# One more key and value group made early, the last block of one thread split by batch, and a new written-out order

## The chip, the cores and the metric

The kernel runs on one core of one Trainium2 chip. The time is device microseconds of one execution. The engines are PE (matmul), DVE (vector), ACT (activation functions), POOL (GpSimd) and SP, which here only issues transfers. Each engine works through its own instructions strictly in the order in which the program holds them, and waits on semaphores for the others. All data are float32; the profile records two PE passes for each float32 matmul.

## The reference

Eight batches of 128 tokens with 256 features pass four transformer blocks, one after the other; a context of the same shape is read by the cross-attentions.

```python
# L0: cross-attention to ctx (16 heads of 16), MLP with tanh gelu
x = x + attn(ln(x), ctx) ; x = x + gelu_tanh(ln(x) @ fc) @ proj
# L1: the context is the "x" of a perceiver block, the stream its latents:
#     keys and values from ctx and the stream together, masked; rms norm, MLP
# L2: twice, i = 1, 2: cross-attention with 16 heads of 128 each
h  = ln_i(x)
q, k, v = h @ wq_i + bq_i, ctx @ wk_i + bk_i, ctx @ wv_i + bv_i     # 256 -> 2048
k, v = concat(k, bias_k_i), concat(v, bias_v_i)                     # one learned key
x  = x + softmax(q k / sqrt(128)) v @ wo_i + bo_i
x  = x + gelu_erf(ln(x) @ w_fc1) @ w_fc2                            # MLP m2
# L3: causal self-attention (a4), cross-attention (a5), MLP with tanh gelu (m3)
x  = x + attn(ln1(x), ln1(x), mask) ; x = x + attn(ln2(x), ctx) ; x = x + mlp(ln3(x))
```

## The kernel before, in words

**Threads.** The batches are dealt to four threads of two batches each, T0 to T3. `blocks(T)` (L1362) is the whole life of a thread: attention a0 and MLP m0 (L0), a1 and m1 (L1), the wide attention twice (L2, `wide_attention`, L1163), m2, then a4, a5 and m3 (L3), and the store of its rows. T2 starts when T0 has left L1, T3 when T1 has left L1 and T0 has left its wide attentions. So the narrow blocks of one thread, which need much of DVE and ACT, stand beside the wide attention of another, which needs mostly PE.

**The wide attention.** `group(T, i, hg)` (L1232) makes four of the 16 heads: `queries` and `keys_values` (L1172) project, two heads to a product of 256 columns; values are one 128x512 product for a batch. Keys go to "kb" buffers (20), values to "vw" (4). `after_scores` (L1302) is the softmax of one batch's four heads in a "t" buffer (7 of them, 128x516, shared with the narrow attentions), the transposes, the weighted values and the output product. Keys and values need only the context. `AHEAD` (L63) names the groups whose keys and values a thread makes at its very start, beside a0 and m0; the `loader` (L510) fetches their weights right after those of a0. A thread may hold four weight buffers of 512 KB (`NW`), all threads eleven.

**Norms.** `normed` and `norm` (L569, L585) make the statistics, and `root` (L608): ten tiny DVE operations that compute the reciprocal square root; then the scaling (either ACT or DVE), transposes on PE through a "tl" bank, and the copy out. POOL adds the bias row to x.

**Products.** `proj`, `product` and `taken` (L541 to L712): a product takes one of two "mm" PSUM banks, PE fills it, then ACT or DVE empty it and the bank is free. `mlp` (L717) does this with gelu on ACT. Scores of the narrow attentions take the four "sc" banks; small transposes and softmax products the two "tl" banks. In L3, `by_pairs` (L1041) makes the softmax with rows of four exponentials on ACT, each with an accumulated sum; in L0 and L1, `by_keys` (L916) uses maxima per key (the tiles "mp") instead. At most two narrow attentions are under way at a time (`attn_lock`).

**What sets the order.** Nothing is ordered at run time. While the program is built, class `Plan` (L83) plays the threads as coroutines: each operation asks for an engine with an urgency (the table `U`, plus the thread's lateness for the stage from `LATE`, smaller is sooner); when the planned engine is free, the most urgent operation gets it and is written to that engine's instruction list. `_weight` (L263) holds the planned duration of each kind of operation, `dma` (L412) that of a transfer. So costs, urgencies and latenesses alter the order of the instructions and nothing else. When PE has nothing to do in the plan and its planned clock is about to fall, `idle_work` (L397) puts in a matmul of the identity with itself, "idle-filling matmul" below, whose result nobody reads.

Every engine call goes through one wrapper, so all of them carry line L333 in the profile; tiles tell the operations apart. Names: "w" weights, "hT" normalised and transposed rows, "ctxT" the transposed context, "kb" keys, queries and hidden rows, "at" and "attnT" attention outputs, "xn" normalised rows, "st", "mv", "rv", "ry", "rz" the parts of the norm, "sm" and "mn" softmax sums and maxima.

Of the kernel before, what the change touches and what calls it, by code (L numbers as in the profile page):

```python
# [18 lines left out]
P = 128  # L19
# [43 lines left out]
AHEAD = [[(1, 0), (1, 1)], [], [], []]  # L63
U = {'take': -0.44, 'taken': -1, 'norm': -0.47, 'mask': 0.26, 'k': 2.41, 'q': 1.79, 'v': 2.5, 'by key': 0.5, 'softmax': 2.46, 'weights': 1.63, 'pairs': 0.75, 'out': 1.79, 'mlp norm': 0.75, 'mlp 1': 4.29, 'mlp 2': 1.92, 'wide norm': -1, 'wide k': 3.49, 'wide q': 4.0, 'wide v': 4.43, 'wide s': 1.19, 'wide': -0.3, 'ahead': 4.34, 'load': -0.39}
LATE = [(1.69, 2.1, 2.22, -0.57, 1.75, 0.04, 2.53, 1.2, 4.53, 1.81), (12.77, 7.95, 10.47, 7.4, 1.7, -1, 8.48, 3.14, 7.46, 6.32), (3.27, 2.62, 3.89, 0.6, 2.14, -1, 4.58, 4.56, 5.62, 0.26), (0.03, 1.69, 0.31, 1.11, 0.24, 3.18, -0.81, -0.64, -0.7, 1.05)]
# [17 lines left out]
class Plan:  # L83
# [12 lines left out]
    def __init__(self):  # L96
        self.now = 0
        self.seq = 0
        self.events = []
        self.asked = []  # L100
        self.until = {e: 0 for e in self.SEEN}
        self.weight, self.shared, self.wrote = 0, False, []
        self.idle_work = None
        self.both_until = {"DVE": 0, "POOL": 0}
        self.clock = Clock()
        self.count = 0
        self.log = []
        self.table = None
        self.dma_until = 0
        self.live = {}  # L110
# [152 lines left out]
def _weight(eng, name, args, kw):  # L263
# [3 lines left out]
    n = max(sizes)  # L267
# [21 lines left out]
    if eng == "DVE":  # L289
        if name == "tensor_scalar" and n == 4 and len(aps) == 2 and len(args) > 5:  # L290
            return 145, False
        if name == "reciprocal":
            return 65 + 6.25 * n, False
        if name in ("bn_stats", "bn_aggr"):
            return (330 if name == "bn_stats" else 150), False
        if n <= 8:
            return 68, False
        if name in ("tensor_scalar", "tensor_copy") and on_sbuf:
            return 75 + 0.8 * n + 55 * by_part, True
        two = name in ("tensor_tensor", "scalar_tensor_tensor") and sum(  # L300
            x.space == bass.MemoryType.SB and x.free_size() > 1 for x in aps[1:]) == 2
        return 72 + 1.03 * n + 55 * by_part, two
# [35 lines left out]
class Engines:  # L338
    def __init__(self, nc, plan):
        self.tensor, self.vector = Engine(nc.tensor, plan, "PE"), Engine(nc.vector, plan, "DVE")  # L340
        self.scalar, self.gpsimd = Engine(nc.scalar, plan, "ACT"), Engine(nc.gpsimd, plan, "POOL")
        self.sync = nc.sync


def op(eng, f, lat=None, table=None):
    return ((eng, 480 if eng == "SP" else 0, f, lat, table),)
# [8 lines left out]
def four_blocks(ctx: ExitStack, tc: tile.TileContext, a: dict, out: bass.AP):  # L355
# [56 lines left out]
    def dma(f, kb_, early):  # L412

        yield op("SP", lambda: f(nc.sync)) + (op("ACT", lambda: f(nc.scalar)) if early else ())
        plan.dma_until = max(plan.dma_until, plan.now) + kb_ * 2.8
        yield plan.dma_until - plan.now + 2300
# [36 lines left out]
    class Thread:  # L453
        def __init__(self, h, b0, nb):
            self.h = h
            self.nb, self.nt = nb, nb * P
            self.batches, self.tokens = slice(b0, b0 + nb), slice(b0 * P, (b0 + nb) * P)
            self.x = new(const, [P, nb, D], f"x{h}")
            self.ctx = ctxT[:, :, self.tokens]
            self.ready = Event()  # L460
            self.row_in = Event()
            self.w_slots = Slots(NW)
            self.w = {}
            self.w_in = {}
            self.late = 0.0
            self.ahead = {}

# [42 lines left out]
    def loader(T):  # L510
        names = list(weight_list())
        first = {f"l{i}{hg}{x}" for i, hg in AHEAD[T.h] for x in "kv"}
# [23 lines left out]
    def drop(T, n=1):  # L536
        plan.put(T.w_slots, n)
        plan.put(w_slots, n)
# [46 lines left out]
    def norm(T, src, e, w, b, adds, rows, hT, ready, row_done, urgency):  # L585
# [4 lines left out]
        else:  # L590
# [17 lines left out]
            def root():  # L608
# [11 lines left out]
                if b is not None:  # L620
                    nc.vector.tensor_tensor(z, mean, v, ALU.mult)

# [540 lines left out]
    def wide_attention(T, i):  # L1163
        hT, hT_in = yield from normed(
            T, T.x, 1e-5, f"L2_ln{i}_scale", f"L2_ln{i}_offset", [(T.x, T.x, f"L2_bo{i}")], U["wide norm"] + T.late)
        for hg in range(4):
            ends = yield from group(T, i, hg, hT, hT_in)
# [4 lines left out]
    def keys_values(T, i, hg, step_back):  # L1172

        n = f"l{i}{hg}"
        ks, vs = [], []
        bv = []
# [4 lines left out]
        def keys():  # L1181
# [3 lines left out]
            for m in range(0, 4, 2):  # L1185
                yield (kb_slots, 2)
                two = [kb(), kb()]
# [15 lines left out]
        def values():  # L1203
# [3 lines left out]
            for b in range(nb):  # L1207
                yield (v_slots, 1)
                t = new(act, [P, 512], "vw", bufs=4)
# [20 lines left out]
        return ks, vs, k_in, v_in  # L1230

    def group(T, i, hg, hT, hT_in):  # L1232
# [32 lines left out]
        ks, vs, k_in, v_in = T.ahead.pop((i, hg), None) or keys_values(T, i, hg, late)  # L1265
# [3 lines left out]
        for b in range(nb):  # L1269
# [9 lines left out]
            ends.append(spawn(after_scores(T, i, hg, b, s, vs, v_in[b], n), U["wide"] + late, Plan.SEEN["PE"]))  # L1279
        plan.put(kb_slots, 8)  # L1280
# [21 lines left out]
    def after_scores(T, i, hg, b, s, vs, v_in, n):  # L1302
# [59 lines left out]
    def blocks(T):  # L1362
# [6 lines left out]
        for i, hg in AHEAD[h]:  # L1369
            T.ahead[i, hg] = keys_values(T, i, hg, LATE[h][0] + U["ahead"])  # L1370
# [27 lines left out]
        T.late = LATE[h][7]  # L1398
# [4 lines left out]
        T.late = LATE[h][8]  # L1403
# [4 lines left out]
        T.late = LATE[h][9]  # L1408
# [66 lines left out]
```

## Time and profile before

| | us |
|---|---|
| median of 3 runs | 1197.38 (1197.1 to 1198.49) |
| the profiled execution | 1198.46 |
| its span | 1196.7, so 1.76 lie outside |
| PE, DVE, ACT, POOL busy | 1145.7, 751.2, 574.1, 339.1 |
| granted PE clock, mean | 0.996 |
| first wide query product of T0 | 177.3 |
| end of T3's wide attention, end of its m2 | 1028.4, 1069.4 |
| one table load on ACT, count | 1.283, 50 |
| 512 KB of weights, issue to landing | 3.9 |

A matmul's length in the profile is its way through the array; the next one starts sooner, so for PE the distance from start to start tells the cost. A line of the view by stretch has the time from and to, its length, then busy time and instructions of PE, weight loads, DVE, ACT and POOL, the granted clock, the share of time that the DMA engines were busy, and GB/s. Times count from the start of the span.

### The profile page before, as it was taken

What the parts mean: (1) busy time and instruction counts of PE and PEld (TensorE: products, weight loads), DVE (VectorE), ACT (ScalarE), POOL (GpSimd) and SP (SyncE); (2) the same over time, 40 slices, a digit from 0 to 9 for tenths busy, and PEclk for the clock granted to TensorE, in tenths of its full rate; (3) what the DMA queues carried; (4) which work ended last, traced back from release to release, by engine and by line L of the source; (5) the groups of instructions that cost most, each with busy time, mean ns of one, the idle gap of its engine ahead of it and who ended that gap; (6) DMA issues with size and microseconds to landing.
All of it is one profiled execution on the core that took longest, in us unless ns stands there. A gap on an engine that the chain in (4) does not pass through costs nothing.

```text
span 1196.7 us, 21922 instructions
## 1 busy us (share of the span) xinstructions
PE 1145.7 (96%) x8318; PEld 937.0 (78%) x8318; DVE 751.2 (63%) x1943; ACT 574.1 (48%) x1448; POOL 339.1 (28%) x392
## 2 busy tenths in 40 slices
PE   8899889999999999999999999999999999999888
PEld 7577668788887777787888897787887887877767
DVE  7755668744554867977872365626568456778872
ACT  4344544452433345675653243434436334686972
POOL 4021111112221210360611022211217212475870
PEclk9899999999999999999999999999999999999999
DMA  9423131336444324343324644543544543432120
GB/s 319 131 84 116 54 98 58 125 117 191 131 147 132 107 90 130 103 133 97 118 85 130 190 145 121 161 157 125 145 130 141 159 133 111 134 100 67 51 80 18
DMA packets 107321, 145.59 MB, mean 122 GB/s; under 512 B 6736, under 2 KB 66256, under 8 KB 107216
## 3 DMA queue, kind: packets, MB, share of 16 engines
q1 hardware_dynamic: 105984, 143.02, 38.3%
q8 instruction: 66, 1.08, 0.4%
q10 hardware_dynamic: 1232, 1.16, 0.3%
q14 instruction: 39, 0.32, 0.1%
HBM read 143.11 MB, written 1.05 MB: 120 GB/s over the span
## 4 chain that ended last, share of the span: by engine, by line
PE 78%; DVE 13%; ACT 5%; issue 1%; POOL 1%; DMA 0%; ACTq 0%; POOLq 0%; DVEq 0%
PE mm L333 57%; PE tl L333 17%; PE sc L333 5%; DVE t L333 2%; DVE mp L333 1%; DVE rz L333 1%; ACT t L333 1%; ACT pt L333 1%; DVE mn L333 1%; ACT q L333 1%; POOL t L333 1%; DVE ry L333 1%; DVE q L333 1%; ACT L333 1%; DVE rv L333 1%
## 5 line engine op out<-in xcount | busy, mean ns | idle before, releaser
L333 PE MATMUL mm<-hT,w 128*128 128x256 f32 x1216 | 286.7, 382 | 5.9 <-ACT kb L333 1.8
L333 PEld LDWEIGHTS mm<-hT,w 128*128 128x128 f32 x1216 | 223.7, 190 | 46.1 <-issue 6.4
L333 POOL TENSOR_TENSOR t<-t,sm 128x512 f32<-128x512 f32 x128 | 132.2, 1043 | 296.6 <-DVE sm L333 215.2
L333 PE MATMUL mm<-ctxT,w 128*128 128x256 f32 x608 | 144.0, 381 | 2.2 <-DVE k L333 2.1
L333 PE MATMUL mm<-w,ctxT 128*128 128x512 f32 (+1 forms) x352 | 143.8, 537 | 1.2 <-ACT k L333 0.7
L333 PEld LDWEIGHTS mm<-ctxT,w 128*128 128x128 f32 x608 | 111.5, 190 | 19.2 <-issue 4.2
L333 DVE TENSOR_TENSOR x<-mm,x 128x256 f32<-128x256 f32 (+1 forms) x96 | 49.0, 511 | 119.6 <-PE mm L333 118.9
L333 PE MATMUL mm<-w,at 128*128 128x256 f32 x512 | 120.4, 380 | 1.9 <-ACT kb L333 1.9
L333 PE MATMUL mm<-w,kb 128*128 128x256 f32 x512 | 117.5, 381 | 0.0
L333 POOL TENSOR_TENSOR x<-x,row 128x512 f32<-128x512 f32 x40 | 50.8, 1270 | 230.5 <-ACT xn L333 118.5
L333 PEld LDWEIGHTS mm<-w,at 128*128 128x128 f32 x512 | 94.8, 190 | 17.5 <-issue 2.6
L333 PEld LDWEIGHTS mm<-w,kb 128*128 128x128 f32 x512 | 95.3, 190 | 13.9 <-issue 1.1
L333 ACT ACTIVATE t<-t,mn 128x128 f32<-128x128 f32 x256 | 99.1, 390 | 11.6 <-DVE mn L333 10.3
L333 ACT ACTIVATE at<-tl,cols 128x128 f32<-128x128 f32 x224 | 64.0, 369 | 62.2 <-PE tl L333 61.9
L333 PEld LDWEIGHTS mm<-w,ctxT 128*128 128x128 f32 x352 | 63.4, 190 | 37.8 <-issue 31.4
L333 POOL TENSOR_TENSOR bv<-bv,bb 128x512 f32<-128x512 f32 x32 | 40.7, 1271 | 178.6 <-DMA bb<-in_L_bias_v 153.7
L333 POOL TENSOR_TENSOR t<-t,mask 128x512 f32<-128x512 f32 x64 | 79.8, 1273 | 26.3 <-DVE t L333 22.4
L333 PE MATMUL tl<-ident,t 128*128 128x128 f32 x512 | 75.6, 275 | 9.0 <-POOL t L333 4.0
L333 PEld LDWEIGHTS tl<-ident,t 128*128 128x128 f32 x512 | 60.3, 141 | 25.9 <-POOL t L333 12.9
L333 ACT ACTIVATE t<-t 128x516 f32<-128x516 f32 x64 | 40.5, 633 | 79.4 <-DVE t L333 79.1
L333 ACT ACTIVATE kb<-mm,cols 128x256 f32<-128x256 f32 x128 | 53.0, 472 | 52.0 <-PE mm L333 51.7
L333 DVE TENSOR_TENSOR vw<-mm,bv 128x512 f32<-128x512 f32 x64 | 43.7, 684 | 46.8 <-PE mm L333 46.6
(121 smaller groups left out, 1797.8 us busy)
## 6 DMA issues: line engine op xcount, KB each, us to landing
w<-in_L_wk SPq DMA_DIRECT2D x32, 512.0 KB, 3.7
w<-in_L_wv SPq DMA_DIRECT2D x32, 512.0 KB, 3.9
w<-in_L_wq SPq DMA_DIRECT2D x32, 512.0 KB, 3.7
w<-in_L_wo SPq DMA_DIRECT2D x32, 512.0 KB, 3.9
bv<-in_L_bv SPq DMA_DIRECT2D x32, 256.0 KB, 4.9
bb<-in_L_bias_v SPq DMA_DIRECT2D x32, 256.0 KB, 5.5
w<-in_L_mlp_w SPq DMA_DIRECT2D x16, 512.0 KB, 3.9
w<-in_L_w_fc SPq DMA_DIRECT2D x16, 512.0 KB, 4.3
```

What stands on the lines that cost most here:

```text
L333: return f(*args, **kw)
```

## The change

Four things are altered together.

1. T0 makes a third group ahead: (1,0), (1,1) and (1,2) instead of (1,0) and (1,1). The keys and values of the first lie in softmax buffers ("t"): two halves of two for the four keys, two for the values. That group goes first in the wide attention, and its buffers return to the softmax then.
2. T3's last block is no longer run for both its batches together: two `Part` objects of one batch each go through a4, a5 and m3 as threads of their own, with their own latenesses, on the same weights, which come free when both have used them. Each part stores its own rows.
3. Planned costs: `root` +250 ns, small DVE operations with per-partition operands +55 ns each, SP's 480 ns by way of the wrapper, and a transfer holds SP in the plan when the planned queue is more than 3.5 us behind.
4. `U` and `LATE` have new numbers. With 3 this gives every engine another order throughout.

```diff
-AHEAD = [[(1, 0), (1, 1)], [], [], []]
+BY_BATCH = (3,)
+AHEAD = [[(1, 0, 't'), (1, 1), (1, 2)], [], [], []]
-U = {'take': -0.44, 'taken': -1, 'norm': -0.47, ..., 'softmax': 2.46, ..., 'ahead': 4.34, 'load': -0.39}
+U = {'take': -0.96, 'taken': -1, 'norm': -0.44, ..., 'softmax': 1.5, ..., 'ahead': 4.98, 'load': 1.96}
-LATE = [(1.69, 2.1, 2.22, ...), (12.77, 7.95, 10.47, ...), (3.27, ...), (0.03, 1.69, 0.31, 1.11, 0.24, 3.18, -0.81, -0.64, -0.7, 1.05)]
+LATE = [(1.35, 1.68, 3.62, ...), (11.94, 11.74, 9.81, ...), (3.87, ...), (0.03, -1, -0.09, 1.11, 0.24, 3.18, -1, -0.77, -0.4, 2.02, -0.33, 0.64, 3.94)]
...
         if n <= 8:
-            return 68, False
+            return 68 + 55 * max(0, len(aps) - 2) * (name == "tensor_scalar"), False
...
+        def sync():
+            f(nc.sync)
+            plan.weight += max(0, plan.dma_until - plan.now - 3500)
+
-        yield op("SP", lambda: f(nc.sync)) + (op("ACT", lambda: f(nc.scalar)) if early else ())
+        yield op("SP", sync) + (op("ACT", lambda: f(nc.scalar)) if early else ())
...
+    class Part:
+        def __init__(self, T, b):
+            self.h, self.nb, self.nt = T.h, 1, P
+            b0 = T.batches.start + b
+            self.batches, self.tokens = slice(b0, b0 + 1), slice(b0 * P, (b0 + 1) * P)
+            self.x = T.x[:, b : b + 1, :]
+            self.ctx = ctxT[:, :, self.tokens]
+            self.ready, self.row_in = T.ready, T.row_in
+            self.w, self.w_in, self.of, self.dropped = T.w, T.w_in, T, 0
...
     def drop(T, n=1):
+        if isinstance(T, Part):
+            T.dropped += n
+            least = min(p.dropped for p in T.of.parts)
+            T, n = T.of, least - T.of.dropped
+            T.dropped = least
         plan.put(T.w_slots, n)
         plan.put(w_slots, n)
...
                 nc.vector.tensor_scalar(y, v, -1.0, None, ALU.mult)
                 if b is not None:
                     nc.vector.tensor_tensor(z, mean, v, ALU.mult)
+                plan.weight += 250
...
-        for hg in range(4):
-            ends = yield from group(T, i, hg, hT, hT_in)
+        ends = []
+        for hg in sorted(range(4), key=lambda hg: not (T.ahead.get((i, hg)) or [False])[-1]):
+            ends += yield from group(T, i, hg, hT, hT_in)
...
-                yield (kb_slots, 2)
-                two = [kb(), kb()]
+                if in_t:
+                    yield (t_slots, 1)
+                    t = new(act, [P, 516], "t", bufs=NT_)
+                    two = [t[:, : 2 * P], t[:, 2 * P : 4 * P]]
+                else:
+                    yield (kb_slots, 2)
+                    two = [kb(), kb()]
...
-                yield (v_slots, 1)
-                t = new(act, [P, 512], "vw", bufs=4)
+                yield (t_slots if in_t else v_slots, 1)
+                t = new(act, [P, 516], "t", bufs=NT_)[:, :512] if in_t else new(act, [P, 512], "vw", bufs=4)
...
-        plan.put(kb_slots, 8)
+        plan.put(kb_slots, 4 if in_t else 8)
+        if in_t:
+            plan.put(t_slots, 2)
...
-        T.late = LATE[h][7]
+        T.parts = [Part(T, b) for b in range(nb)] if h in BY_BATCH else []
+        for e in [spawn(last_block(p, LATE[h][7 + 3 * i : 10 + 3 * i]), 0) for i, p in enumerate(T.parts)] or [
+                spawn(last_block(T, LATE[h][7:10]), 0)]:
+            yield e
+
+    def last_block(T, late):        # a4, a5, m3 and the store, as before, for a thread or a part
+        x, nb = T.x, T.nb
+        T.late = late[0]
```

## The prediction

> **What bounds the kernel now.** Of the page I read the engines' busy times, the slices and the chain that ended last; then busy time by stretch, then timelines.
>
> ```profile
> span 1196.7 us, 21922 instructions
> PE 1145.7 (96%) x8318; PEld 937.0 (78%) x8318; DVE 751.2 (63%) x1943; ACT 574.1 (48%) x1448; POOL 339.1 (28%) x392
> PE   8899889999999999999999999999999999999888
> PEclk9899999999999999999999999999999999999999
> PE 78%; DVE 13%; ACT 5%; issue 1%; POOL 1%; DMA 0%; ACTq 0%; POOLq 0%; DVEq 0%
> ```
>
> PE is the bound, full except at both ends. But busy is not useful: idle-filling matmuls and a half clock are in it. I measure with pitches from PE's timeline in a dense place (start, length, engine, what):
>
> ```profile
> 703.63 1.06 PE L333 MATMUL tl<-kb,kb 128*128 128x128 f32 x8
> 704.52 1.89 PE L333 MATMUL mm<-ctxT,w 128*128 128x256 f32 x8
> 706.25 1.89 PE L333 MATMUL mm<-hT,w 128*128 128x256 f32 x8
> ```
>
> Start to start, eight 256-column matmuls take 1.73 us and eight 128-column ones 0.89 us; in the same way a 512-column one takes 0.43 us and the 32-row score and value forms some 0.035 us per 128 columns. With the counts of the costliest groups that makes about 1103 us of useful matmul, so 1196.7 - 1103 = 94 us of the span are lost to PE. Walking PE's order with these pitches (call the useful time so far W) and subtracting W from each start shows where. Busy times by stretch (time, PE, PEld, DVE, ACT, POOL, clock, DMA share):
>
> ```profile
> 0.00:70.00 70.00, 60.89 (x580) 47.13 (x581) 51.54 (x147) 30.07 (x52) 15.44 (x35) 0.95 0.61 200
> 70.00:177.30 107.30, 96.50 (x889) 77.13 (x888) 66.40 (x195) 49.23 (x85) 16.69 (x28) 0.98 0.29 93
> 200.00:388.00 188.00, 187.12 (x1055) 155.36 (x1054) 97.68 (x248) 75.72 (x173) 37.91 (x49) 1.00 0.43 136
> 388.00:570.00 182.00, 175.44 (x1547) 141.16 (x1546) 143.36 (x365) 102.90 (x211) 46.45 (x54) 1.00 0.37 112
> 570.00:985.00 415.00, 412.18 (x2463) 339.78 (x2462) 230.21 (x571) 173.87 (x462) 108.70 (x117) 1.00 0.45 139
> 985.00:1069.40 84.40, 81.85 (x554) 68.31 (x553) 58.57 (x145) 50.70 (x151) 37.11 (x36) 1.00 0.35 110
> 1069.40:1125.60 56.20, 48.65 (x497) 39.40 (x496) 46.98 (x128) 45.20 (x165) 41.62 (x41) 1.00 0.25 78
> 1125.60:1196.70 71.10, 62.42 (x477) 51.38 (x475) 38.45 (x111) 36.92 (x139) 31.90 (x32) 1.00 0.15 45
> ```
>
> Lost by then: 20.8 us at 70, 41.4 at 177.3 (first wide query product of thread 0), 46.4 at 388, about 61 at 640, 62.4 at 985, 66.6 at 1069.4 (end of thread 3's m2, W = 1002.9), 89.6 at 1160; then PE is dense to its last matmul, and 4 us of add and store follow. The wide stages lose nothing; the front loses 41, 388 to 640 loses 14.5 where DVE is 79% busy, the last block loses 27.
>
> In the tail the other engines are full, one after the other:
>
> ```profile
> 1110.00:1120.00 10.00, 7.69 (x106) 6.06 (x102) 7.84 (x18) 9.95 (x42) 9.48 (x10) 1.00 0.36 120
> 1140.00:1150.00 10.00, 8.27 (x138) 6.45 (x139) 9.86 (x20) 6.86 (x28) 8.51 (x8) 1.00 0.45 144
> 1150.00:1160.00 10.00, 7.47 (x71) 5.44 (x70) 8.92 (x32) 8.73 (x42) 8.13 (x8) 1.00 0.01 2
> ```
>
> **The change, part by part.** The changed program's order on each engine stands fixed in its text, so W can be walked for it too. Useful work hardly changes: 32 projection matmul pairs of 256 columns become 64 of 128, 128 x 0.1135 - 64 x 0.216 = +0.7 us. ACT gets 9 table loads more. The rest is where things stand.
>
> *Third early group.* Two key products (1.73 each) and two value products (1.72 each), 6.9 us of PE, leave the wide stage for W = 34 to 43.5, about where before loses 9.4 us (44 to 61 us: PE waits for a0's key maxima on DVE). Thread 0's m0 begins at W = 46.0 instead of 41.3, its first wide query at 141.5 instead of 135.9. If the front's DVE-bound chain keeps its clock time, that is 5.6 us less lost. Beside it: four key copies of 0.48 and two value adds of 0.68 on DVE or ACT (3.3 us); 1 MB of weights and 0.5 MB of bias rows more on SP's queue ahead of m0's weights. At the 340 GB/s of 10 to 30 us, where the queues are full, 1.5 MB is 4.4 us; from 40 to 60 us the DMA share is 0.3 or less, which hides it. The softmax buffers that it takes are unused until the wide stage's first scores. Ends: 0 (all of it pushed into the chain) and -6.9; taken -5.6, since the DMA cover is in the rows.
>
> *Thread 2's start.* The new order has ten idle-filling matmuls in a row at W = 203.7: PE waits for the x add, statistics, root, normalisation and transposes ahead of thread 2's m0, while thread 1's m1 is held back; before, this place (about 250 us) is dense. By DVE rows: 0.69 + 2 x 0.42 + 2 x 0.17 + 0.26 + 1.85 (ten root steps) + 2 x 0.43, and 0.45 of transposes: 5.2 us. Ends: +2.2 (ten fillers at 0.22 start to start, as in the run of five at 136.3) and +8; taken +5.2.
>
> *Middle.* Thread 0's a5 and m3 move later (m3 from 582-620 to 787-820 in W). Priced by rows, the DVE work put beside W = 340 to 580 falls from 198 to 164 us, beside the stretch that lost 14.5; it goes to where before DVE is 55% busy and nothing is lost. Losses there follow DVE's queue; I take -6. Ends -12 and +3 (a small loss as at 430 to 490). This also holds the dearer price of the small operations, which alters nothing but order.
>
> *Ahead of the tail.* In W = 900 to 1000 the new order has ACT 79 us (before 63) and DVE 81 (before 69). Before, the stretch W = 1000 to 1060, with such density, lost 14 in 60. Thread 3's m2 ends at W = 1019.2 instead of 1002.9. Taken +3; ends 0 and +8.
>
> *Last block batch by batch.* What follows m2's end: 84.4 us of PE work instead of 100.0, some 20 softmax rows by pairs of heads instead of 28 (each 2.3 us of ACT for four exponentials with their read-outs), 77 us of DVE instead of 97. A part's norm, queries and scores need no second batch, but they are twice as many links, on in-order queues: thread 1's and 2's m3 products hold both product banks, and their gelu evacuations stand on ACT behind the other part's exponentials. Followed by hand, part 0's a4 output comes 59 us after m2's end (before 56), and the end 122 after it (before 127.3): 38 us lost. By density (each engine's work beside PE's, and no filler after W = 1053 where before has eight) 18 lost, so 102. I take the row nearest, the old tail's own loss per work, 27.3 x 84.4/100 = 23.0, so 107.4; ends 102 and 122. A weight's buffer now comes free when both parts have used it, which costs nothing: nothing is loaded after m3's weights. The last add is of one batch (0.42 instead of 0.69), the store halved; I leave both out.
>
> Five of the new table loads lie past W = 1000, 6.4 us of ACT by this row:
>
> ```profile
> 1104.73 0.19 ACT L333 ACTIVATION_READ_ACCUMULATOR t<-t,mn 128x1 f32 x1
> 1104.93 1.28 ACT L333 ACT_TABLE_LOAD   x1
> 1106.23 1.57 ACT L333 ACTIVATE kb<-mm,cols 128x256 f32<-128x256 f32 x4
> ```
>
> The load starts 0.01 us after the read-out ends, so I count 1.28 each. The Trainium skill ("ScalarE: Activation LUTs", What ACT_TABLE_LOAD costs) adds a drain of about 1.38 us to every switch; by it the five would be, as an estimate, 13.3 us. This row shows no such gap, and the sum leaves it out.
>
> **The sum.** Lost at m2's end: 66.6 - 5.6 + 5.2 - 6 + 3 = 63.2. m2 ends at 1019.2 + 63.2 = 1082.4; with 107.4 the span is 1189.8, 6.9 below 1196.7. The profiled execution took 1198.46 (1.76 outside its span), 1.1 over the median of the runs; 6.9 below the median is 1190.5. Less than 0.2% (2.4 us) can't be told from no change.
>
> **Rivals.**
>
> *The tail goes by its chain* (slower): 122 instead of 107.4, hence 1190.5 + 14.6 = 1205. For it: ACT 9.95 and DVE 9.86 of 10 us in the old tail, five more table loads there, and 16 us more PE work ahead of m2's end, so that less is left to fill the waits. Against: 20% less DVE work, and fillers from two threads. It decides from a tail of about 114 us.
>
> *The front pays for its group* (no change): 1.5 MB ahead of m0's weights and 3.3 us of copies keep m0 back by what was saved: 1190.5 + 5.6 = 1196.1. For it: DMA share 0.98 and more from 10 to 30 us. Against: that share falls to 0.3 after 40.
>
> *The middle clears up and the tail packs* (faster still): -12 there and a tail of 102: 1190.5 - 6 - 5.4 = 1179.
>
> *The clock in the new gap*, a small one: in 50 to 55 us the clock is 0.58 after PE's 1.62 busy of 5. If the ten fillers at W = 203.7 don't hold it, 3 to 4 us more go at half speed, +2; in the upper bound. The skill ("TensorE: Matmul & The Clock Gate", What's actually happening) puts the fall at an idle window of about 3.4 us, which agrees with that row.
>
> **Chances.** Forecast 0.37 (1184 to 1195), faster still 0.13, no change 0.12, tail by its chain (with dearer fronts) 0.38. Faster 0.50, same 0.12, slower 0.38. Range: a tenth off each end of these cases, 1178 to 1207.
>
> **What would show it.** Thread 0's first wide query still near 177 us: the group was free; near 183: the second rival. PE idle about 5 us with fillers near 250: the gap. Less than 10 us lost from W = 340 to 640: the middle. From m2's last matmul to the end 107 or 122 decides the sign; in the latter, ACT at 9.9 of 10 with PE waiting for gelu and weights. I would be most wrong if the new tail waits on a transfer: the last m3's second weights are issued behind other stores on SP, 4 to 6 us ahead of use, against 3.9 us to land.

## The result: slower by 0.6%, with the losses of the front unchanged

The changed kernel takes 1205.62 us (median of 4 runs, 1205.02 to 1206.74) against 1197.93 for the kernel before on the same chip (4 runs, 1197.1 to 1199.36). The ratio is 1.0062, with a 95% interval of 1.0049 to 1.0074. The forecast was 1190.5 and faster. The profiled execution took 1205.02 us, 1.82 of them outside the span.

These lines of the changed kernel's page answer to those shown of the kernel before: span and instructions, busy time by engine, PE's busy tenths, its granted clock in tenths, and the chain that ended last.

```profile
span 1203.2 us, 22211 instructions
PE 1153.7 (96%) x8402; PEld 943.6 (78%) x8402; DVE 745.5 (62%) x1967; ACT 593.5 (49%) x1486; POOL 342.4 (28%) x403
PE   8998898999999999999999999999999999999898
PEclk8999999999999999999999999999999999999899
PE 77%; DVE 13%; ACT 6%; issue 2%; DMA 2%; POOL 1%; SPq 0%; ACTq 0%; DVEq 0%; POOLq 0%
```

By these lines alone hardly anything has changed: PE is still the bound and as full as it was. The difference must be read by stretch. Busy time by stretch of the changed kernel (time, PE, PEld, DVE, ACT, POOL, clock, DMA share, GB/s); the cuts are thread 0's first wide query (182.9), W = 340 and 580 (395 and 647.3), and the end of thread 3's m2 (1096.7):

```profile
0.00:70.00 70.00, 62.95 (x531) 47.76 (x532) 46.90 (x139) 26.26 (x47) 17.74 (x38) 0.95 0.70 220
70.00:182.90 112.90, 99.94 (x939) 80.22 (x938) 71.69 (x203) 52.07 (x92) 16.63 (x28) 1.00 0.29 86
182.90:260.00 77.10, 72.12 (x670) 60.35 (x669) 52.09 (x121) 34.36 (x68) 11.19 (x12) 1.00 0.24 78
395.00:647.30 252.30, 246.75 (x1837) 200.27 (x1836) 172.01 (x440) 138.42 (x344) 78.55 (x86) 0.99 0.41 125
985.00:1096.70 111.70, 106.88 (x858) 88.50 (x857) 82.34 (x216) 75.02 (x259) 65.14 (x67) 1.00 0.33 105
1096.70:1203.20 106.50, 95.19 (x817) 79.37 (x815) 68.57 (x218) 67.36 (x230) 49.64 (x56) 0.96 0.21 63
```

The kernel before, from W = 340 to 580:

```profile
386.40:640.90 254.50, 246.37 (x2133) 199.96 (x2132) 195.89 (x513) 143.45 (x326) 75.78 (x83) 1.00 0.37 112
```

PE's order was walked again with the same pitches; "lost" is the start of an instruction minus W, the useful time ahead of it. "W = 220" means the last instruction that starts with W up to 220.

| lost up to | before | after | the stretch's own change |
|---|---|---|---|
| first wide query of thread 0 | 41.4 (at 177.3) | 41.4 (at 182.9) | 0 |
| W = 220 | 46.0 | 51.7 | +5.7 |
| W = 580 | 60.9 | 67.3 | +0.7 |
| end of m2 of thread 3 | 67.0 (at 1069.4) | 77.5 (at 1096.7) | +4.1 |
| last matmul | 89.6 | 96.2 | -3.9 |

Together 6.6 us more are lost, and 0.7 us of useful work is added; the add and store behind the last matmul are 0.8 us shorter, which gives the 6.5 us between the two spans. The new tail is better than the old one. What makes the kernel slower is that the third early group, which should have made the front shorter, brought nothing by the first wide query, and that the middle gained nothing as a whole, while the wait at thread 2's start and the denser work ahead of the tail came as priced.

### The profile page after: what moved, and what is told of

Same layout as the page of the kernel before. It is cut to its first block, busy times and chain, and to the rows that moved or that the text cites. A ratio compares the mean times of both kernels' runs of the same rounds, so it can differ in the third digit from the quotient of the medians.

```text
span 1203.2 us, 22211 instructions
## 1 busy us (share of the span) xinstructions
PE 1153.7 (96%) x8402; PEld 943.6 (78%) x8402; DVE 745.5 (62%) x1967; ACT 593.5 (49%) x1486; POOL 342.4 (28%) x403
## 4 chain that ended last, share of the span: by engine, by line
PE 77%; DVE 13%; ACT 6%; issue 2%; DMA 2%; POOL 1%; SPq 0%; ACTq 0%; DVEq 0%; POOLq 0%
PE mm L334 56%; PE tl L334 16%; PE sc L334 4%; DVE mp L334 2%; DVE tm L334 2%; DVE rz L334 1%; DVE t L334 1%; ACT t L334 1%; ACT pt L334 1%; POOL t L334 1%; ACT q L334 1%; DVE ry L334 1%; DVE st L334 1%; ACT kb L334 1%; ACT L334 1%
## 5 line engine op out<-in xcount | busy, mean ns | idle before, releaser
L334 PE MATMUL mm<-hT,w 128*128 128x256 f32 (+1 forms) x1272 | 290.1, 375 | 7.7 <-ACT kb L334 1.6
L334 PEld LDWEIGHTS mm<-hT,w 128*128 128x128 f32 x1272 | 229.8, 192 | 46.9 <-issue 4.4
L334 PE MATMUL mm<-ctxT,w 128*128 128x256 f32 (+1 forms) x616 | 146.8, 383 | 5.3 <-DMA mask<-in_mask_b 3.0
L334 POOL TENSOR_TENSOR x<-x,row 128x512 f32<-128x512 f32 (+1 forms) x43 | 51.3, 1193 | 243.6 <-ACT xn L334 152.3
L334 PEld LDWEIGHTS mm<-w,at 128*128 128x128 f32 x512 | 94.2, 190 | 14.6 <-ACT q L334 1.1
L334 ACT ACTIVATE at<-tl,cols 128x128 f32<-128x128 f32 x212 | 60.3, 368 | 43.6 <-PE tl L334 42.0
L334 DVE TENSOR_SCALAR kb<-mm,cols 128x256 f32<-128x256 f32 x66 | 31.2, 482 | 77.3 <-ACT kb L334 71.5
```

The costliest lines, as they stand in the source:

```text
L334: return f(*args, **kw)
```

## The experiments

Each kernel was timed beside the kernel before on the same chip; its median there lay between 1198.5 and 1199.6 us. "Front loss" is the time lost at thread 0's first wide query: 41.4 both before and after. It comes from one profile of each kernel. Profiles of the same PE order differ in it: 44.2 in e4 against 41.4 in the kernel before, 42.1 in e3 against 41.4 in the changed one.

### The first transfers (e1)

In the changed kernel the first useful matmul starts at 8.93 us, in the one before at 6.51: the mask of a0 (many small packets) is issued second on SP, ahead of the first weights. e1 gives thread 0's first transfers the old places and alters nothing else:

```diff
-            ends = [spawn(load(at(t), src, ..., early), U["load"] - 2 * early) for at, src in pieces]
+            ends = [spawn(load(at(t), src, ..., early, (nc.sync, nc.scalar)[n] if early else None, ...),
+                          U["load"] - 2 * early) for n, (at, src) in enumerate(pieces)]
...
-        yield spawn(load(raw, a[name][:, T.tokens]..., 64 * nb), -1)
+        yield spawn((load_after if T.h == 0 and name == "mask_b" else load)(raw, ..., 64 * nb), -1)
```

> The changed kernel, with the order on PE, DVE, ACT and POOL untouched; only thread 0's first transfers go out as before the change: on SP the context, the key and query weights, and then the 32 KB mask; on ACT x, the columns, the value and output weights. In the changed kernel's trace the mask stands second on SP, the first useful matmul starts at 8.9 us instead of 6.5 and the first query product at 19.1 instead of 13.1. Theory A (the early group did fill the front's holes, and the late start took the gain back): the first query product comes near 14 us, thread 0's first wide query near 178.5 instead of 182.9, and the end some 4 us sooner, about 1201.5. Theory B (the front's chain on DVE is longer for the early group, the start does not matter): the first wide query stays within 1.5 us of 182.9, the time near 1205.

Measured: 1206.68 us, ratio 1.0054 (1.0038 to 1.007). The first useful matmul starts at 6.64, yet the first scores at 23.80 (after: 23.74) and m0 at 64.23 (64.16); front loss 43.2, with the first wide query at 184.6. So nothing is won, as theory B said. The 2.3 us were waiting time, and PE now waits later. Part of what it waits for is on DVE; the timeline of the changed kernel there (start, length, engine, operation; in brackets the idle time before it and what ended it):

```profile
7.48 0.29 DVE L334 TENSOR_SCALAR mask<-mask 128x256 f32<-128x256 uint8 x1
15.18 0.60 PE L334 MATMUL tl<-ident,xn 128*128 128x128 f32 x4
15.96 0.75 DVE L334 BATCH_NORM_STATS2 st<-x 128x6 f32<-128x256 f32 x2 [6.29 <-DMA x<-in_x]
17.05 0.99 DVE L334 TENSOR_SCALAR hT<-tl,cols 128x256 f32<-128x256 f32 x2
19.68 0.48 DVE L334 SCALAR_TENSOR_TENSOR k<-mm,hs,k 128x256 f32<-128x256 f32 x1
```

Thread 1's statistics stand ahead of thread 0's hT and key copies in DVE's order, and they wait for thread 1's x: DVE stands idle for 6.29 us with thread 0's work behind it. Before, that wait was 0.92 us at 15.28. Not all of the 6.29 us keeps thread 0 back: its own transposes, from which hT is copied, end only at 15.78, so that hT comes 1.3 us late (17.05). In e1 they end at 13.69 and hT starts at 17.11, 3.4 us late.

### Thread 1's first norm behind thread 0's queries (e5)

e1 with thread 1's first norm (statistics, root, scaling) issued after thread 0's first query copies and its transposes after thread 0's first scores:

```diff
-            yield op("DVE", stats)
-            yield op("DVE", root)
+            hold = T.h == 1 and w == "L0_ln1_w"
+            put = (lambda f: later(plan, f)) if hold else (lambda f: f)
+            yield op("DVE", put(stats))
+            yield op("DVE", put(root))
...
-        yield op("PE", transposes)
+        yield op("PE", later(plan, transposes, LATER_PE) if T.h == 1 and w == "L0_ln1_w" else transposes)
```

> The changed kernel with thread 0's first transfers in their former order and, besides, thread 1's first norm moved: its statistics and root on DVE and its scaling on ACT stand behind the copies of thread 0's first queries instead of before its keys and queries, its transposes on PE behind thread 0's first scores. All else keeps its place. In the changed kernel DVE waits 6.3 us for thread 1's rows (statistics at 16.0 us) with thread 0's normalised rows and keys queued behind. Theory A (this wait is what makes the front late): thread 0's first scores start near 17.5 us instead of 23.7, the first wide query near 178 to 180 instead of 182.9 to 184.6, and the time is 3 to 5 us below that of the kernel with the transfers alone put back (1206.7). Theory B (the lateness is made later, in thread 0's second attention, where thread 1's late first attention shares DVE with it): the first scores come sooner too, but thread 0's m0 and the first wide query stay within 1.5 us of 64.2 and 183 to 185, and the time within 2 us of 1206.7.

Measured: 1213.70 us, ratio 1.011 to 1.0138. The first scores come 0.9 us sooner than in e1 (22.88) and everything after that later: m0 at 69.48, front loss 46.9. Neither theory said this. The likely reason, read from the order and not tried alone: thread 1's products stand between thread 0's in PE's order, so that holding back thread 1 holds back thread 0 at the next product. Taking this one wait out of an order made for it did not shorten the front.

### The third group's work left out (e2)

The changed kernel without the work of the third early group: its transfers, products and copies are not issued, and its buffers are filled with zeros on POOL.

```diff
+        out_ = T.h == 0 and (i, hg) == (1, 2)
...
-                        lambda j=j: nc.scalar.activation(two[j][:, :nt], ..., bias=b[:, j : j + 1]),
+                        less(lambda j=j: nc.scalar.activation(two[j][:, :nt], ...), two[j][:, :nt]),
```

> The changed kernel with the third early group's work left out: no transfer of its weights and bias rows, no key and value products (6.9 us of PE), no copies; POOL fills the six buffers with zeros instead, so the attention of that group is not computed rightly. All other instructions keep their order. Theory A (the group only fills holes): the first wide query stays within 1.5 us of 182.9, since PE waits there instead. Theory B (the group lies on the chain of the front): it comes 4 to 7 us sooner, near 177. Both: from there on the losses are those of the changed kernel.

Measured: 1211.67 us, ratio 1.0075 to 1.0123; the first wide query comes at 186.4, 3.6 us later, though 6.9 us of products are gone. Neither theory said this. The reason that it became slower is the clock: without these products PE falls idle and is granted less. Stretches of e2, then of the changed kernel:

```profile
50.00:60.00 10.00, 6.55 (x49) 5.54 (x50) 6.99 (x10) 0.40 (x1) 0.00 (x0) 0.66 0.16 50
140.00:160.00 20.00, 18.14 (x101) 14.73 (x102) 12.05 (x33) 8.23 (x17) 0.81 (x3) 0.91 0.26 81
```

```profile
50.00:60.00 10.00, 10.00 (x68) 7.06 (x67) 8.79 (x20) 1.72 (x4) 0.00 (x0) 1.00 0.96 309
140.00:160.00 20.00, 18.85 (x140) 15.39 (x139) 10.49 (x29) 10.24 (x20) 0.00 (x0) 1.00 0.34 106
```

0.66 instead of 1.00 over 10 us is 3.4 us of clock. Up to the first wide query the mean clock is 0.95 in e2 and 0.98 in the changed kernel, some 9 and 3.5 us of clock. With that taken off both, e2 would be there about 2 us sooner, as an estimate. So the group costs the front at most some 2 us of its 6.9, no more than two profiles of one order differ by, and the second rival ("the front pays for its group") does not account for the 5.6 us.

### Filling the idle places of the front (e6)

The kernel before, with 46 more idle-filling matmuls at seven places of its front and all else in order:

```diff
+    FILLS = {13: 11, 16: 5, 21: 3, 25: 4, 27: 4, 29: 14, 32: 5}
...
+                for _ in range(more):
+                    tc.nc.tensor.matmul(p, lhsT=ident, rhs=ident, start=True, stop=True)
```

> The kernel before, with 46 more idle-filling matmuls at seven places of the front where its trace has PE waiting 0.9 to 3.5 us (46, 58, 137, 140, 162, 168 and 195 us), each 0.22 us or a little more; no other instruction moves. Its trace has the granted clock at half from 47.3 to 54.2 and from 173.6 to 177.0 us, 10.3 us in all, which cost PE 5.2 us. If the clock falls because PE is idle, these stretches go to full clock: the first wide query comes near 173 instead of 177.3 and the time is 3 to 5 us below the kernel before. If the half-clock stretches come of something else, or the fillers come in the way, the time is the same or up to 3 us longer.

Measured: 1198.16 us, ratio 0.9988 (0.9979 to 0.9997). From 50 to 55 us the clock is now 1.00, where it was 0.58, and the first wide query comes 3.2 us sooner (174.1). At m2's end 1.5 us of that are left, and in its profile none at the end, because the clock was 0.91 from 1100 to 1120 (before 1.00). So the clock does fall because PE is idle, which agrees with what the Trainium skill says in "TensorE: Matmul & The Clock Gate", What's actually happening. Work that nobody reads buys a little here.

### The group alone, and the planned costs (e8, e10, e11, e12, e13)

These five take the front apart. But for e8's group they differ only in what is planned, and hence in the order. e8 is the kernel before with the third group alone:

```diff
-AHEAD = [[(1, 0), (1, 1)], [], [], []]
+AHEAD = [[(1, 0, 't'), (1, 1), (1, 2)], [], [], []]
```

> The kernel before with the third early group in softmax buffers and nothing else of the change: costs, urgencies, latenesses and the last block as before, so that the order is a new one from the start on. Theory A (the group fills the front's holes): the first wide query stands 6.9 us later in useful work and at 177 us give or take 2, and the loss up to there is 35 to 37 us instead of 41.4. Theory B (the group costs the front its own length): at 182 us or later. The rest of this order was never tuned to it; what it loses later, 20 us or more, is the price of one part without the other.

Measured: 1226.36 us, ratio 1.0213 to 1.025. Front loss 34.1, 7.2 us less than the kernel before, where the prediction had 5.6. Part of that is the clock: in e8 it is 1.00 up to 258 us, in the kernel before 0.91 from 40 to 80 us and 0.97 from 126 to 183; e6 had 3.2 us from fillers alone. Beside e6, with 38.2 lost, 4.1 us are left for the move itself. The gain is given back, first at thread 2's start: its m0 comes at 253.3 us (before 256.2), and 4.2 us are lost from W = 204 to 210, where before nothing is. The rest goes in a tail whose order nobody tuned for it (57.8 lost after W = 580, before 28.7).

e10 adds the new planned costs to e8; e11 is the changed kernel with all the old ones.

```diff
-        self.dma_until = 0
+        self.dma_until = 2500
...
-            return 68, False
+            return 68 + 55 * max(0, len(aps) - 2) * (name == "tensor_scalar"), False
...
+            plan.weight += max(0, plan.dma_until - plan.now - 3500)
...
+                plan.weight += 250
```

> The third early group with the new planned costs, but the former urgencies and latenesses, and the last block whole. With the group alone the first wide query stood at 175.4 us with 34.1 us lost (changed kernel: 182.9, 41.4). If the new costs of the small operations and transfers spoil the front, it stands here with 40 us lost or more; if the new urgencies and latenesses do, with 36 or less. What comes after the front is an order that nobody tuned.

> The changed kernel with the planned costs of before (roots, small operations and transfers as they were counted), so third group, new urgencies and latenesses and the split last block. If the new urgencies and latenesses spoil the front, the first wide query stands with 40 us lost or more here too; if the new costs do, with 36 or less.

Measured: e10 1217.18 us (1.014 to 1.0175) with a front loss of 47.0; e11 1216.97 us (1.0139 to 1.0174) with 36.8. Their ends are those of untuned tails. The fronts tell what is wanted: with the old costs the changed kernel loses 4.6 us less there, and the new costs alone put 12.9 on e8. About half of the 12.9 can be clock: it is 0.66 from 20 to 30 us, 0.77 from 100 to 110 and 0.89 from 110 to 120 in e10, and 1.00 all the way in e8.

e12 and e13 are the changed kernel with one half of the old costs each:

```diff
-            return 68 + 55 * max(0, len(aps) - 2) * (name == "tensor_scalar"), False
+            return 68, False
...
-                plan.weight += 250
```

```diff
-        self.dma_until = 2500
+        self.dma_until = 0
...
-            plan.weight += max(0, plan.dma_until - plan.now - 3500)
+            plan.weight += 0
```

> The changed kernel with the old planned costs of root and of the small DVE operations, the new ones of SP kept. Thread 0's first wide query came with 41.40 us lost in the changed kernel and with 36.82 where all planned costs are old. Theory R (the dearer root is planned into a later gap, so that other DVE work goes ahead of it): 36 to 38 lost here. Theory S (SP's costs, which set when transfers are issued, move the front): 41 to 42 here. Neither alone: about 39. The end says nothing here, since the tail's latenesses were made for the other order.

> The other half: the old planned cost of SP, the new ones of root and of the small DVE operations. Theory R: 41 to 42 us lost at thread 0's first wide query, with the root of that norm again 4 to 5 us behind its statistics on DVE. Theory S: 36 to 38. Neither alone: about 39.

Measured (single runs of 1221.97 and 1213.25 us): front loss 38.8 in e12 and 44.1 in e13. e12 loses 1.9 us more than e11 in the first 30 us (its clock is 0.84 from 10 to 20 us and 0.88 from 20 to 30, in e11 1.00). The 38.8 alone would also fit "neither alone"; what decides is a later stretch, picked after the runs. From W = 100 to the first wide query e12 loses 9.7, e11 9.6, and with the new cost of the root the changed kernel 14.2 and e13 13.2. The other kernels with the third group fall on the same sides: 8.8 in e8 (old cost), 14.3 in e3, e5 and e10 and 15.8 in e1 (new cost). The clock is 1.00 from 127 to 174 us in all of these but e1 (0.96); behind that only e13 has a fall worth naming (0.83 from 170 to 180). Theory R holds, if not to its number: it is the dearer norm, that is the root and the small DVE operations, whose costs were not tried apart. DVE's timeline shows how, at the norm ahead of thread 0's first wide query. The changed kernel, from that norm's statistics to the root's last operations:

```profile
167.60 0.75 DVE L334 BATCH_NORM_STATS2 st<-x 128x6 f32<-128x256 f32 x2
168.60 0.17 DVE L334 TENSOR_SCALAR rv<-mv 128x2 f32<-128x2 f32 x1
168.67 0.29 DVE L334 TENSOR_SCALAR mask<-mask 128x256 f32<-128x256 uint8 x1
...
170.82 2.35 DVE L334 TENSOR_REDUCE mp<-sc 128x4 f32<-128x1024 f32 x2
173.09 0.15 DVE L334 TENSOR_SCALAR ry<-rv 128x2 int32<-128x2 int32 x1
...
174.72 0.16 DVE L334 TENSOR_TENSOR rz<-mv,rv 128x2 f32<-128x2 f32 x1
```

And e12, with the old cost of the root:

```profile
167.69 0.75 DVE L334 BATCH_NORM_STATS2 st<-x 128x6 f32<-128x256 f32 x2
168.68 0.17 DVE L334 TENSOR_SCALAR rv<-mv 128x2 f32<-128x2 f32 x1
168.76 0.41 DVE L334 TENSOR_SCALAR xn<-x,ry,rz 128x256 f32<-128x256 f32 x1
169.08 0.16 DVE L334 TENSOR_SCALAR ry<-rv 128x2 int32<-128x2 int32 x1
...
170.73 0.15 DVE L334 TENSOR_TENSOR rz<-mv,rv 128x2 f32<-128x2 f32 x1
170.80 2.35 DVE L334 TENSOR_REDUCE mp<-sc 128x4 f32<-128x1024 f32 x2
```

The statistics end at the same time. With the old cost the root starts 0.4 us after rv, with the new one 4.5 us after it, behind another thread's mask counts and key maxima (mp), and ends 4.0 us later. The normalised rows, their transposes and the first wide query all follow from it; what each later place in the order adds was not taken apart.

### The last block as a whole (e3), and split in the old order (e4)

e3 is the changed kernel with thread 3's last block run for both batches together; e4 is the kernel before with the split alone, and latenesses chosen for it.

```diff
-BY_BATCH = (3,)
+BY_BATCH = ()
-LATE = [..., (0.03, -1, -0.09, 1.11, 0.24, 3.18, -1, -0.77, -0.4, 2.02, -0.33, 0.64, 3.94)]
+LATE = [..., (0.03, -1, -0.09, 1.11, 0.24, 3.18, -1, -0.64, -0.7, 1.05)]
```

```diff
+BY_BATCH = (3,)
-LATE = [..., (0.03, 1.69, 0.31, 1.11, 0.24, 3.18, -0.81, -0.64, -0.7, 1.05)]
+LATE = [..., (0.03, 1.69, 0.31, 1.11, 0.24, 3.18, -0.81, -0.99, -6.37, 3.85, 2.81, -1.31, 3.94)]
```

> The changed kernel with thread 3's last block for both batches together, with the three latenesses it had before the change; the order is the same up to that block. If splitting by batch is what shortened the stretch from thread 3's m2 to the end (106.5 us for 84.4 us of PE work, after 127.3 for 100.0), this one takes 115 us or more there and the time is about 1214 or above. If the fillers from threads 1 and 2, held back by the new latenesses, did it, it takes 104 to 110 us and the time stays within 3 us of 1205.6.

> The kernel before, with thread 3's last block split into two parts of one batch and nothing else; the order is the same up to the end of thread 3's m2. Theory A (the split shortens the tail by itself): from m2 to the end less than 124 us instead of 127.3, the time below 1195. Theory B (the split makes twice as many links, and pays only with enough work of other threads beside it): 130 us or more, the time above 1200.

Measured: e3 1220.33 us (1.0151 to 1.0194), e4 1223.90 us (1.0182 to 1.0216). From m2's end to the end of the span, e3 and then e4; beside the 106.50 after and 127.30 before:

```profile
1100.60:1219.50 118.90, 106.08 (x827) 88.06 (x825) 60.59 (x174) 60.13 (x208) 47.87 (x47) 0.96 0.17 53
```

```profile
1071.30:1224.40 153.10, 130.19 (x1103) 107.48 (x1101) 93.35 (x280) 91.48 (x326) 75.54 (x81) 0.95 0.18 52
```

In the new order the split is worth 12 us; in the old order it costs 26. Each was tried with one set of latenesses only, so that the two numbers hold for these. The order up to m2's end is the same within each pair. In e4 the key product of thread 2's a5 moves from 1094.8 to 1118.1, and the output product of that a5 from 1149.7 to 1166.5. The code says why (this was argued, not tried alone): at most two narrow attentions run at a time, and the two parts take both places, where before thread 3 took one and thread 2 the other. In the new order threads 1 and 2 bring mostly m3 to the tail.

### A shorter root (e7, e9, e14)

In e7 the changed kernel's root has three operations instead of ten, in the same places (both refinement steps are left out, so that the norms are only rough). In e9 (the kernel before) and e14 (the changed one) it has six, with one refinement step of third order; the step of second order ahead of it is left out. In effect, for e9 and e14 (the constant ahead of the root, 256/9, becomes 64/9; the plan still counts ten operations):

```diff
                 nc.vector.tensor_scalar(y.bitcast(I32), v.bitcast(I32), -0.5, float(0x5F3759DF), ALU.mult, ALU.add)
                 nc.vector.tensor_tensor(z, y, y, ALU.mult)
                 nc.vector.tensor_tensor(z, z, v, ALU.mult)
-                nc.vector.scalar_tensor_tensor(y, z, -3.0, y, ALU.add, ALU.mult)
-                nc.vector.tensor_tensor(z, y, y, ALU.mult)
-                nc.vector.scalar_tensor_tensor(z, z, 0.25, v, ALU.mult, ALU.mult)
                 nc.vector.scalar_tensor_tensor(z, z, -10 / 3, z, ALU.add, ALU.mult)
-                nc.vector.scalar_tensor_tensor(v, z, 5.0, y, ALU.add, ALU.mult)
-                nc.vector.tensor_scalar(y, v, -1.0, None, ALU.mult)
+                nc.vector.scalar_tensor_tensor(y, z, 5.0, y, ALU.add, ALU.mult)
                 if b is not None:
-                    nc.vector.tensor_tensor(z, mean, v, ALU.mult)
+                    nc.vector.scalar_tensor_tensor(z, mean, -1.0, y, ALU.mult, ALU.mult)
```

> The changed kernel with every root cut from ten small DVE operations to three (the refinement of the reciprocal root is left out, so the norms are only roughly right): seven operations of some 0.19 us less in each of 39 norms, about 1.3 us a norm and 50 us of DVE, 7% of its work; order and all else stay. Theory A (losses of PE in the middle follow the load of DVE): the 15.5 us lost between W = 220 and 580 fall by 4 us or more, and the whole by 10 us or more. Theory B (they are single waits of other chains, set by the order): the middle loses within 2.5 us of 15.5, and the whole falls by what the norms on the chain of the front, of the gap ahead of thread 2's m0 and of the tail are shorter, 1.3 us for each of some eight, less what the clock takes back.

> The kernel before with a shorter root: the first of its two refinement steps is left out and the last copy folded in, six small DVE operations instead of ten (the remaining step is of third order; the reciprocal root is then right to about 1e-4), with every other instruction in its place. The root cut to three operations took 12.5 us off the changed kernel, 1.8 us for each operation of the norm. If that carries over, four operations less take about 7 us: 1191 to 1193, with 3 us or more of it between W = 340 and 580. If the kernel before waits for other things (its fronts gained 3 us from fillers and gave most of it back), the gain is below 3 us.

> The changed kernel, its order unaltered, with the root of six operations (one refinement step less). In the kernel before it took the time from 1198.5 to 1190.1, 8.4 less. If the change's loss lies where root's length doesn't matter, 8 less here too, near 1197.5, and 7 to 8 behind the kernel before with the short root. If the change loses because its order puts roots on the path, more comes back: 1192 to 1194, 2 to 4 behind.

Measured: e7 1193.11 us (0.9936 to 0.9973), e9 1190.05 us (0.9918 to 0.9951), e14 1198.91 us (0.9992 to 1.0013). e9 beats both kernels. Its page, then that of e14 (whose profiled execution, 1195.1 us, is its shortest):

```profile
span 1189.3 us, 21778 instructions
PE 1144.8 (96%) x8318; PEld 939.1 (79%) x8318; DVE 729.3 (61%) x1799; ACT 573.1 (48%) x1448; POOL 339.3 (29%) x392
```

```profile
span 1193.3 us, 22056 instructions
PE 1148.6 (96%) x8402; PEld 941.4 (79%) x8402; DVE 725.0 (61%) x1811; ACT 593.4 (50%) x1486; POOL 342.9 (29%) x403
```

e14 lies 8.9 us above e9 (8.5 when each is taken against the kernel before on its own chip), as the changed kernel lies 7.7 above the one before. So the change's loss is not one that shorter roots undo, although the roots themselves lie on the path in both. Lost in W = 220 to 580: after 15.6, e14 11.2, e7 10.2; before 14.9, e9 15.0. Some of this is clock, which the runs of the same orders with the long root take out: e1 and e3, at full clock there, lose 14.6 and 14.9, and e6, with the same 0.90 from 390 to 400 us and 0.93 from 400 to 410 as e9, loses 15.9. So the shorter root takes some 3.5 us from the changed order's middle and 0.9 from the old one's; e9 gains in the front (2.3) and past W = 860 (5.0) instead. By the terms set for e7, its 5.4 us in the middle and 12.5 in all speak for theory A, that the loss follows DVE's load. e9 speaks against: there the middle, with DVE the busier, gained least, though 3 us or more were expected of it from W = 340 on.

One such place of the changed kernel, near 500 us:

```profile
499.90 0.16 DVE L334 TENSOR_TENSOR rz<-ry 128x2 f32<-128x2 f32 x1
500.23 1.26 POOL L334 TENSOR_TENSOR bv<-bv,bb 128x512 f32<-128x512 f32 x1
500.29 1.22 DVE L334 SCALAR_TENSOR_TENSOR ry<-rz,ry 128x2 f32<-128x2 f32 x1
501.55 0.16 DVE L334 TENSOR_TENSOR rz<-ry 128x2 f32<-128x2 f32 x1
...
502.66 0.60 ACT L334 ACTIVATE xn<-x,rz,ry 128x256 f32<-128x256 f32 x1 [1.62 <-DVE rz L334]
503.28 1.28 ACT L334 ACT_TABLE_LOAD   x1
504.57 0.84 ACT L334 ACTIVATE kb<-mm,cols 128x256 f32<-128x256 f32 x2
505.46 2.90 PE L334 MATMUL mm<-hT,w 128*128 128x256 f32 x7 [1.60 <-ACT kb L334]
```

ACT waits 1.62 us for the root, then loads a table, and only then empties the bank for which PE waits. With the shorter root e14 loses 1.1 us from W = 440 to 460, the changed kernel 3.8; of the 2.7 between them 1.7 is the clock, 0.83 from 500 to 510 us in the changed kernel and 1.00 in e14. e1 and e3, with the long root and full clock there, lose 2.1.

## Why the prediction was wrong, step by step

Lost at m2's end was to be 63.2 and was 77.5; the terms, with what they measured:

- *Third early group, -5.6: measured 0.* This is one of the two steps that failed. It was priced as work moved into idle time, and the move itself did much as it should: 7.2 us less lost in the old order (e8), some 4 of them beside a kernel whose clock is full too (e6), at a cost of 2 us at most (e2). What the step left out is that the same change reorders the front. The dearer planned norms took 4.6 back (36.8 to 41.4, e11 to after; e12 and e13 name them, all of it behind W = 100). New urgencies and first transfers may have taken 2.7 (34.1 to 36.8, e8 to e11), which is no more than two profiles of one order differ by. The prediction said of those costs that they alter "nothing but order", put them under the middle, and didn't follow the front's order on DVE. A reading beside it was wrong too, without weight here: the DMA share is 0.3 or less only from 40 to 55 us, and 0.68 from 55 to 60.
- *Thread 2's start, +5.2: measured +5.7.* Right, in place and size (the rows of the prediction's sum add to 5.3). e8 shows 4.2 of it in the old order too: thread 2's m0 comes at 253 to 256 us in before, e8, e11 and after, whatever useful work stands ahead of it. This reads as if the chain of the narrow blocks up to there sets the time, and what is made ahead is missing as cover while PE waits for it; it was not tried alone.
- *Middle, -6: measured +0.7 from W = 220 to 580* (-2.2 from 340 on, +2.9 ahead of it, whose cause stays open). The other step that failed: "Losses there follow DVE's queue". DVE's work did fall, by 24 us where 34 were priced (before 195.89 of 254.5 us, after 172.01 of 252.3, in the stretch to W = 580), and the loss fell by 2.2. At the one place shown, near 500 us, it isn't a queue that is full but a row of single links: norm, root, ACT's table load, an emptied bank; that the other places are like it was not shown. Before, three bins of 20 lose 8.3 of the 14.5 (W = 340 to 360 and 420 to 460); after, 440 to 460 and 480 to 500 lose 6.1 (1.7 of it clock), and small waits the rest.
- *Ahead of the tail, +3: measured +4.1.* Right.
- *Last block, 107.4: measured 106.5.* Right in size: a split that loses per work what the old tail lost. There is luck in it. The number is a proportion taken between 102 and 122, the chain followed by hand gave 122, and e4 shows the same split 26 us dearer in another order. The rival that would have given 1205, "the tail goes by its chain" with 122, has the number and not the cause: it was to show as ACT at 9.9 of 10, and ACT is busy 67.36 of 106.50 us there, at most 8.73 of any 10 between 1100 and 1180.
- *The test for the second rival* ("near 183: the second rival") misled as well: the first wide query is at 182.9, and the group cost 2 us at most all the same. It lay at W = 141.5 instead of 135.9, so an unchanged loss gives this time by any cause.

The terms' errors are 5.6 + 0.5 + 6.7 + 1.1, with 0.4 for reading 66.6 where the same walk gives 67.0 at m2's last matmul: 14.3 of lost time. The sum had the right places; its two gains were counted where a stall was seen, without asking what the new order would put at that stall.

## What to carry to other kernels

- Where an order is written out from planned costs, a changed cost is a changed order. Before crediting a gain, follow the first engine of the chain (here DVE, from statistics to root to scaling) through the new order at the place where the gain is to be seen.
- An average of busy time does not price a stall. From W = 340 to 580 PE lost 14.5 us beside a DVE that was 77% busy, and 12.3 beside one that was 68% busy; two or three short places made about half of it. Shortening one kind of link in the whole kernel (the root, by four operations of 0.2 us) gave 8.4 us, more than the whole change was meant to give.
- Several tuned parts belong together: the split saves 12 us in one order and costs 26 in the other, so it couldn't be judged alone here.

## What the runs showed of the hardware

- Removing work can cost time. With 6.9 us of products left out, PE's clock fell to 0.66 over 10 us, and the front became 3.6 us longer. Differences between profiles come in such pieces: 0.91 over 20 us is 1.8 us. e3 has the changed kernel's order up to m2's end, yet reached it 4 us later, with 0.91 from 180 to 200 and 0.95 and 0.96 from 240 to 280, where the changed kernel's profile shows 1.00; that one has 0.83 from 500 to 510, where e3 has 1.00, so that the clock is about half of the 4 us. Among profiles of the same order, 2 to 4 us tell nothing.
- A tiny DVE operation can wait for POOL. The operation at 500.29 above takes 1.22 us instead of 0.16: POOL's add began 0.06 us ahead of it and ended at 501.49, the DVE operation at 501.51. Such delays add up to 7.4 us over 15 norm operations of the changed kernel, and to 13.5 us over 22 of the one before (each one's length beyond 0.17). The Trainium skill says in "SBUF — State Buffer", Who interferes with whom, that the two engines share a pair of ports, which the one that comes first holds for its whole instruction; these rows agree.
